# Root finder on POOL ahead of the products of queries and sums, differences of weights at other places, and two more chunks turned on the tensor engine

## The chip, the cores and the metric

The kernel runs on one core of one Trainium2 chip. The metric is the device time of one execution in microseconds (us); the time of a kernel is the median over its runs. The core's engines each work through an instruction queue of their own, in order: TensorE (PE in the profile, with its weight loads as PEld), VectorE (DVE), ScalarE (ACT), GpSimd (POOL), and SyncE (SP), which here only issues DMAs.

## The reference

The input is x of 4 sequences of 2048 positions with 512 features, in float32. Two layers are added to it, each behind a layer norm.

- Attention: `xn = layernorm(layernorm(x)) * ln_g + ln_b`, then queries, keys and values `xn @ W_qkv + b_qkv`, and a gate `sigmoid(layernorm(x) @ W_gate + b_gate)`, divided by its mean over the features. Queries and keys are multiplied by the gate, cut into 16 heads of 32, and turned into `relu(.)**2 + 1e-5`. The attention is linear and causal: at each position the state grows by `k v^T` and the sum of keys by `k`; the output is `q @ state / (q @ sum + 1e-5)`, and then `@ W_proj + b_proj`.
- Feed-forward: `P = layernorm(x) @ U1` (rank 128), `H = gelu(P @ V1 + b1)` (2048 wide), `Q = H @ U2`, and `x + Q @ V2 + b2`.

## The kernel before, in words

The 8192 positions are cut into 64 chunks of 128 (`NC`); chunk c is a tile of 128 positions by 512 features. 16 chunks make a sequence (`SEQ`). The order of the work on every engine is written out by hand: `tc.manual_schedule()` keeps the order in which the program issues it, and waits between engines come from the data and from the tiles' buffers. What is issued earlier on an engine's queue runs earlier on that engine, and a waiting instruction holds all behind it.

After a start in which chunks 0 to 3 are treated by themselves, the main loop takes two chunks in each of 30 steps, c = 4, 6, ..., 62, with e = c - 1 the odd chunk of the pair before. A step issues, in this order:

1. `gates_and_values(c, ...)`: gates and values of chunks c and c + 1. Products of a pair are made with seven half products instead of eight (`half_product`, the matmuls of L426), for which sums and differences of the activations (`combinations`, `combos`, on POOL) and differences of the weights (`difference`, L1014, slots T1 to T4 of the tiles `wgv`, `wqk` and `wp`) are needed.
2. `scores_in_step(e)`: 32 small products (L618) and four masks on VectorE (`a`, L628).
3. `queries_and_keys(c, ...)`: queries and keys of the pair, their squares on ACT, their turning to features first: a transpose in blocks of 32 on VectorE (L286, `blocks_q`, `blocks_k`), a DMA to DRAM (L302) and DMAs back (L307), all through SP. POOL adds to them at L523, L535 and L570.
4. `pump(1)`: the feed-forward of the pair c - 4, c - 3 is a list of 21 pieces, `rest`, of which `pump` issues some: `down` (L844, `ps_P`, from the tile `x2T`; `pT` at L855), 18 pieces `both(f)` (hidden product L859, gelu on ACT L861, and two pieces later its product into `ps_Q`, L865; the last one copies `ps_Q` to `qs` on VectorE, L878), and two pieces `up` (`ps_u`, L883, x + result at L885, and the output DMA L886).
5. The rest of the attention of e, its output combinations (`outs`, POOL, L756 to L759), and `project_two_in_step(e)`, which ends with the moments of the chunks e - 1 and e (`mv`, L226, L227).
6. `sums_and_products(c)`: VectorE's scan `sums` (L594) over the keys of chunk c, and POOL's product `qsum` of queries and sums (L604).
7. `second_norm([e - 1, e], ...)` on POOL: the factors of the second layer norm of chunks e - 1 and e, and, up to c = 58, also those of the first norm of chunks c + 4 and c + 5. L806 to L810 take the variances from `mv`, `inverse_root_by_steps` (L242 to L250) finds the inverse roots in three rounds of four small instructions, and L260, L261, L357 and L358 make the factors (`shift_f`, `shift_o`, `unscale`). It gives back two closures that are kept in `waiting`.
8. `scores_in_step(c)`, then `denominators_in_step(c)`: POOL's x + bp_row (L982), and VectorE's row from `qsum`: transpose `back` (L640), sum (L642), + eps (L643), reciprocals (L649 to L652), transpose `inv` (L655).
9. `pump(4)`, a closure of `waiting`, `pump(2)`, the other closure. Each normalizes one chunk on ACT (x2, L267), adds b2_row to x on POOL (L824), and turns x2: for the chunks below `NC - 2` as in 3 (`turned_in_quarters`: `blocks_x` on VectorE, the write `dr_x`, four reads into `x2T`), for the last two on TensorE (`features_first`, L276, and an ACT copy, L830); of these the turning is handed back as another closure.
10. The combinations of the next pair on POOL, the remaining pieces of `both`, the rest of the attention of c (products with the state, L690, not for the first chunk of a sequence; with the values, L701; the state's growth, L720; `oT` on VectorE, L664), the pieces `up`, the sums of c + 1 and the first norm of the pair c + 4.

The first step, c = 4, differs: x2 of chunks 0 and 1 are normalized inside `queries_and_keys` (`normalized_first`, behind its first VectorE addition, L504), and the sums of chunk 3 are made inside it too. Ahead of the loop the differences of `wgv` are made on POOL between the projection of chunk 0 and the rest of the attention of chunk 1, and those of `wp` behind the projection of chunk 1. Behind the loop chunk 63, the feed-forward of chunks 60 and 61, the projection of chunks 62 and 63, and their feed-forward follow.

Of the kernel before, what the change touches and what calls it, by code (L numbers as in the profile page):

```python
# [60 lines left out]
def tile_linear_attention_block(  # L61
# [19 lines left out]
    nc = tc.nc  # L81
# [213 lines left out]
    def transfers_back():  # L295
        while back:
            back.pop(0)()
# [137 lines left out]
    def gates_and_values(c, s, meanwhile):  # L435

        a, b = xlT_of[c], xlT_of[c + 1]
        lo, hi = slice(0, NH), slice(NH, NK)
        ps1 = bank(f"ps_g_{c}")
        half_product(ps1, a[:, lo], wgv, B11)  # L440
        t1 = temp(f"g1_{c}")
        nc.scalar.copy(t1, ps1)
        ps2 = bank(f"ps_gu_{c}")
        half_product(ps2, s[:, 1], wgv, T2)
        u2 = temp(f"gu2_{c}")
        nc.vector.tensor_add(u2, ps2, t1)
        ps5 = bank(f"ps_g_{c + 1}")
        half_product(ps5, s[:, 2], wgv, T3)
        u3 = temp(f"gu3_{c}")
        nc.vector.tensor_add(u3, ps5, u2)  # L450
        meanwhile()
        half_product(ps1, a[:, hi], wgv, B21, more=True)
        g0 = new_gate(c)
        gate_input(c, g0, ps1)
        done = [sigmoid_of(c, g0)]
        half_product(ps5, b[:, hi], wgv, T4, more=True)
        g1 = new_gate(c + 1)
        nc.vector.tensor_add(g1, ps5, u2)
        gate_input(c + 1, g1, g1)
        done.append(sigmoid_of(c + 1, g1))  # L460


        loaded = work.tile([P, 1], F32, tag="loaded", name=f"loaded_{c}")
        nc.scalar.activation(loaded, eps_col, AF.Gelu_apprx_tanh)
        ps3 = bank(f"ps_gt_{c}")
        half_product(ps3, s[:, 0], wgv, T1)
        t5 = temp(f"g5_{c}")
        nc.vector.tensor_add(t5, ps3, bqkv_row[:, 2 * D : 3 * D])  # L468
        ps4 = bank(f"ps_v_{c}")
        half_product(ps4, s[:, 3], wgv, B22)  # L470
        v0, v1 = new_values(c), new_values(c + 1)
        nc.vector.tensor_add(v0, ps4, t5)
        nc.gpsimd.tensor_add(v1, u3, t5)  # L473
        nc.gpsimd.tensor_add(v0, v0, u2)
        for n, g in enumerate((g0, g1)):
            gate_factor(*done[n])
            gates[c + n] = g, done[n][1]
        values[c], values[c + 1] = v0, v1
# [108 lines left out]
            bias=eps_col,  # L587
        )

    def sums_of(c, kT, qT):  # L590

        sums = work.tile([P, NK, P + 1], F32, tag="sums", name=f"sums_{c}")
        flat = "p g t -> p (g t)"
        nc.vector.tensor_tensor_scan(  # L594
            sums.rearrange(flat),
            keep.rearrange(flat),
            kT.rearrange(flat),
            0.0,
            ALU.mult,
            ALU.add,  # L600
        )
        state["sums"] = sums
        qs = work.tile([P, NK, P], F32, tag="qsum", name=f"qsum_{c}")
        nc.gpsimd.tensor_mul(  # L604
            qs.rearrange("p k (i t) -> p k i t", t=DH),
            qT.rearrange("p i k t -> p k i t"),
            sums[:, :, 1 : P + 1].rearrange("p k (i t) -> p k i t", t=DH),
        )
        return qs
# [190 lines left out]
    def second_norm(chunks, mv, others=(), mv_others=None):  # L800

        at = slice(chunks[0] % NJ, chunks[-1] % NJ + 1)
        name = str(chunks[0])
        n, m = len(chunks), len(others)
        v = variances(n + 2 * m, f"f{name}")
        nc.gpsimd.tensor_scalar_add(v[:, 0:n], mv[:, at, 1], EPS)  # L806
        if others:
            var = mv_others[:, others[0] % NJ : others[-1] % NJ + 1, 1]
            nc.gpsimd.tensor_scalar_add(v[:, n : n + m], var, EPS)
            nc.gpsimd.tensor_scalar(  # L810
                v[:, n + m :], var, 1.0 + EPS, EPS * EPS, ALU.mult, ALU.add
            )
        rs = inverse_root_by_steps(v, "rs_f", name)
        norm = normalizer(mv[:, at, 0], rs[:, 0:n], f"f{name}", nc.gpsimd)
        if others:
            both_factors(others, mv_others, v[:, n:], rs[:, n:], nc.gpsimd)

        def normalize(n, c):
            b, j = divmod(c, NP)
            if b not in x2T_of:  # L820
                x2T_of[b] = work.tile([P, NP, NQ, NK, DH], F32, tag="x2T", name=f"x2T_{b}")
            xt = x_of[c]
            x2 = normalized(xt, norm, n, f"x2_{c}")
            nc.gpsimd.tensor_add(xt, xt, b2_row)  # L824
            to = x2T_of[b][:, j]
            if c < NC - 2:
                turned_in_quarters(x2, to, f"x2_{c}")
                return None

            return lambda: nc.scalar.copy(  # L830
                to.rearrange("p i k t -> p k i t"),
                features_first(x2, f"ps_x2_{c}").rearrange("p k (i t) -> p k i t", t=DH),
            )

        return [lambda n=n, c=c: normalize(n, c) for n, c in enumerate(chunks)]
# [60 lines left out]
    def pump(n):  # L896
        for _ in range(min(n, len(rest))):
            rest.pop(0)()
# [68 lines left out]
    def new_keys_in_step(c):  # L967
        kT = new_keys(c)
        keys_of(kT, pairs[c][2])
        keys[c] = kT, None  # L970

    def sums_and_products(c):
        if c not in keys:
            new_keys_in_step(c)
        kT = keys[c][0]
        keys[c] = kT, sums_of(c, kT, pairs[c][1])

    def scores_in_step(e):
        return scores_of(e, pairs[e][1], keys[e][0])
# [5 lines left out]
    def rest_of_attention(e, scores, inv):  # L985
        results[e] = weighted(e, scores, pairs[e][1], pairs[e][0], values.pop(e), inv)
# [24 lines left out]
    def difference(w, to, engine):  # L1011

        one, other = {T1: (B12, B11), T2: (B22, T1), T3: (B22, B12), T4: (B21, T2)}[to]
        engine.tensor_sub(w[:, to], w[:, one], w[:, other])  # L1014
# [81 lines left out]
    def scores_of_first():  # L1096
        for turn in turn_xl:
            turn()
        held["scores"] = scores_in_step(0)

    second = queries_and_keys(
        2,
        combos.pop(2),
# [11 lines left out]
    new_keys_in_step(2)  # L1115
    inv = denominators_in_step(1)
    project_in_step(0)
    for to in (T1, T2, T4, T3):
        difference(wgv, to, nc.gpsimd)
    rest_of_attention(1, scores, inv)  # L1120
    sums_and_products(2)
    scores = scores_in_step(2)
    second()
    transfers_back()
    project_in_step(1)
    for to in (T1, T2, T4, T3):
        difference(wp, to, nc.gpsimd)
    inv = denominators_in_step(2)
    waiting += second_norm([0, 1], mv_second)
    rest_of_attention(2, scores, inv)  # L1130
# [2 lines left out]
    for c in range(NJ, NC, 2):  # L1133

        e = c - 1
        for n in (c + 4, c + 5):
            if n < NC:
                load_x(n)
        held = {}

        def denominators():
            held["inv"] = denominators_in_step(e)

        later = c == NJ
        if later:
            gates_and_values(c, combos[c], lambda: new_keys_in_step(e))

            def normalized_first():
                while waiting:
                    waiting.pop(0)()  # L1150
                transfers_back()

            scores = scores_in_step(e)
            second = queries_and_keys(
                c,
                combos.pop(c),
                first=normalized_first,
                queries=lambda: sums_and_products(e),
            )
        else:  # L1160
            gates_and_values(c, combos[c], denominators)
            scores = scores_in_step(e)
            second = queries_and_keys(c, combos.pop(c))

        rest += feed_forward((c - 4) // NP)
        pump(1)
        if later:
            denominators()
        rest_of_attention(e, scores, held["inv"])
        combine_results(e)  # L1170
        features_back()
        second()
        if later:
            for turn in normalize_pair(c + 2):
                turn()
            features_back()
        for n in (c + 4, c + 5):
            first_moments(n)
        pump(4)
        project_two_in_step(e)  # L1180
        transfers_back()
        pump(2)
        sums_and_products(c)
        others = [c + 4, c + 5] if c + 4 < NC else []
        waiting += second_norm([e - 1, e], mv_second, others, mv_first)
        pump(2)


        scores = scores_in_step(c)
        inv = denominators_in_step(c)  # L1190
        pump(4)
        waiting.pop(0)()
        pump(2)
        waiting.pop(0)()
        transfers_back()
        if c + 2 < NC:
            combine(c + 2)
        pump(len(rest) - NP)
        rest_of_attention(c, scores, inv)
        if c + 2 < NC:  # L1200
            pump(len(rest))
            sums_and_products(c + 1)
        for turn in normalize_pair(c + 4):
            turn()
# [76 lines left out]
```

## Time and profile before

| | |
|---|---|
| median of 3 runs | 1830.09 us (1827.73 to 1830.84) |
| the profiled execution: its own time | 1826.79 us |
| the profiled execution: span in the profile | 1825.0 us |
| granted clock of TensorE, mean over the span | 0.997 |
| busy: PE, PEld, DVE, ACT, POOL | 97%, 62%, 72%, 36%, 46% |
| chain that ended last | PE 91%, DVE 4%, ACT, DMA, POOL and issue 1% each |
| one step of the loop, `ps_u` (L883) to `ps_u` | 55.7 us |
| one with the first chunk of a sequence | 55.1 us |

A line of a timeline reads: start in us from the span's beginning, duration, engine, line of the kernel, operation, output <- inputs, shape, how many were merged; in brackets the idle time of the engine ahead of it and what the profile names as its end. TensorE's matmuls are pipelined: 0.59 us stands beside a pair of `ps_h` products, and the next pair starts 0.43 us later. So a loss is read from the distance of the starts. A table of groups gives, behind the bar, the busy time, the mean duration in ns, and the idle time ahead of the group with what ended most of it.

### The profile page before, as it was taken

The numbers are of one execution on the slowest core, as the hardware profiler recorded it, in microseconds if no ns is written. First come the engines' busy times: TensorE is split into PE (matmuls) and PEld (weight loads), VectorE is DVE, ScalarE is ACT, GpSimd is POOL, SyncE is SP. The second block draws the span as 40 slices with busy tenths as digits, with TensorE's granted clock in tenths as the row PEclk, the third lists the DMA queues.
The fourth block names the chain that finished last, engine by engine and source line by source line (L and its number), as shares of the span: only waits on it lengthen the run. The fifth ranks groups of instructions, "written<-read, shape, count | busy, mean of one in ns | idle before, by whom it ended". The sixth has DMA issues, their size and how long they took to land.

```text
span 1825.0 us, 35492 instructions
## 1 busy us (share of the span) xinstructions
PE 1776.5 (97%) x13112; PEld 1133.1 (62%) x13112; DVE 1320.5 (72%) x2579; ACT 659.8 (36%) x1203; POOL 834.6 (46%) x1397
## 2 busy tenths in 40 slices
PE   9989999999999999999999999999999999999998
PEld 4545666656666556666566665566655666655667
DVE  7877777777777777677777777776777777777762
ACT  4323433333333334333333333333333333333333
POOL 3574553444553445544545534455435445344441
PEclk9999999999999999999999999999999999999999
DMA  7123322323323333223233233232233332332220
GB/s 229 60 93 99 111 91 82 102 88 103 105 85 90 99 92 110 92 86 100 87 101 116 77 93 99 87 111 96 84 98 88 99 116 76 94 99 75 87 82 24
DMA packets 286129, 173.79 MB, mean 95 GB/s; under 512 B 134654, under 2 KB 235518, under 8 KB 285828
## 3 DMA queue, kind: packets, MB, share of 16 engines
q1 hardware_dynamic: 284894, 171.51, 30.4%
q8 instruction: 104, 1.70, 0.4%
q14 instruction: 69, 0.57, 0.1%
q10 hardware_dynamic: 1062, 0.01, 0.0%
HBM read 89.68 MB, written 81.79 MB: 94 GB/s over the span
## 4 chain that ended last, share of the span: by engine, by line
PE 91%; DVE 4%; ACT 1%; issue 1%; DMA 1%; POOL 1%; SPq 0%; ACTq 0%; DVEq 0%; POOLq 0%
PE ps_Q L865 13%; PE ps_h L859 12%; PE ps_q L426 11%; PE ps_g L426 11%; PE ps_a L618 4%; PE ps_u L883 3%; PE ps_pt L426 3%; PE ps_p L426 3%; PE ps_t L426 3%; PE ps_k L426 3%; PE ps_v L426 3%; PE ps_u L426 3%; PE ps_gt L426 3%; PE ps_pv L426 3%; PE ps_P L844 3%; PE ps_gu L426 3%
## 5 line engine op out<-in xcount | busy, mean ns | idle before, releaser
L861 ACT ACTIVATE h<-ps_h,b_col 128x256 f32<-128x256 f32 x512 | 227.5, 468 | 288.2 <-PE ps_h L859 288.1
L865 PE MATMUL ps_Q<-h,u_sb 128*128 128x256 f32 x1024 | 304.7, 388 | 25.4 <-ACT h L861 25.4
L859 PE MATMUL ps_h<-pT,v_sb 128*128 128x256 f32 x1024 | 300.5, 385 | 1.6 <-DVE pT L855 1.6
L865 PEld LDWEIGHTS ps_Q<-h,u_sb 128*128 128x128 f32 x1024 | 186.2, 189 | 79.8 <-ACT h L861 57.6
L604 POOL TENSOR_TENSOR qsum<-qT,sums 128x512 f32<-128x512 f32 x64 | 75.4, 1178 | 339.5 <-DVE sums L594 333.1
L859 PEld LDWEIGHTS ps_h<-pT,v_sb 128*128 128x128 f32 x1024 | 189.5, 190 | 32.1 <-DVE pT L855 2.9
L426 PE MATMUL ps_q<-wqk,xlT 128*128 128x512 f32 x372 | 177.9, 601 | 0.0
L628 DVE TENSOR_TENSOR a<-ps_a,causal 128x512 f32<-128x512 f32 x256 | 158.3, 680 | 23.8 <-PE ps_a L618 23.8
L426 PE MATMUL ps_g<-wgv,xlT 128*128 128x512 f32 x360 | 166.2, 597 | 3.6 <-DVE gu L450 3.6
L523 POOL TENSOR_TENSOR u<-u,t 128x512 f32<-128x512 f32 x32 | 40.7, 1272 | 214.2 <-DVE t L521 214.2
L570 POOL TENSOR_SCALAR k<-k 128x512 f32<-128x512 f32 x64 | 96.3, 1505 | 82.9 <-DVE blocks_k L286 82.9
L473 POOL TENSOR_TENSOR v<-gu,g 128x512 f32<-128x512 f32 x30 | 38.1, 1271 | 208.1 <-DVE g L468 208.1
L426 PEld LDWEIGHTS ps_g<-wgv,xlT 128*128 128x128 f32 x360 | 68.7, 191 | 90.2 <-issue 85.2
L426 PEld LDWEIGHTS ps_q<-wqk,xlT 128*128 128x128 f32 x372 | 68.1, 189 | 78.3 <-issue 53.1
L405 ACT ACTIVATE gate<-gate 128x512 f32<-128x512 f32 x64 | 40.3, 630 | 192.7 <-DVE gate L401 192.7
L494 ACT ACTIVATE t<-t,rg 128x512 f32<-128x512 f32 x32 | 23.1, 722 | 215.7 <-DVE t L492 215.7
L226 DVE BATCH_NORM_STATS2 st<-x 128x6 f32<-128x512 f32 x128 | 86.5, 676 | 8.4 <-DMA x<-in_L_attn_x_dram 6.2
L498 ACT ACTIVATE k<-u,rg 128x512 f32<-128x512 f32 x64 | 45.7, 714 | 120.8 <-DVE u L492 120.1
L618 PEld LDWEIGHTS ps_a<-qT,kT 32*128 32x128 f32 x2048 | 63.6, 186 | 33.7 <-issue 31.8
L982 POOL TENSOR_TENSOR x<-x,bp_row 128x512 f32<-128x512 f32 x64 | 81.8, 1278 | 0.0
L824 POOL TENSOR_TENSOR x<-x,b_row 128x512 f32<-128x512 f32 x64 | 80.1, 1274 | 0.9 <-ACT x L267 0.9
L594 DVE TENSOR_TENSOR_SCAN sums<-keep,kT 128x516 f32<-128x516 f32 x64 | 78.5, 1227 | 0.3 <-ACT kT L583 0.3
(196 smaller groups left out, 3607.6 us busy)
## 6 DMA issues: line engine op xcount, KB each, us to landing
x<-in_L_attn_x_dram SPq DMA_DIRECT2D x64, 256.0 KB
dr_q<-blocks_q SPq DMA_DIRECT2D x64, 256.0 KB
dr_k<-blocks_k SPq DMA_DIRECT2D x64, 256.0 KB
qT<-dr_q SPq DMA_DIRECT2D x256, 64.0 KB
kq<-dr_k SPq DMA_DIRECT2D x256, 64.0 KB
out_dram<-x SPq DMA_DIRECT2D x64, 256.0 KB
dr_x<-blocks_x SPq DMA_DIRECT2D x62, 256.0 KB
x2T<-dr_x SPq DMA_DIRECT2D x248, 64.0 KB
```

What stands on the lines that cost most here:

```text
L226: nc.vector.bn_stats(st, src)
L426: nc.tensor.matmul(ps, stationary[:, k, :], w[:, slot, k, :], start=(k == 0 and not more), stop=(k == NH - 1), skip_group_check=True,)
L570: nc.gpsimd.tensor_scalar_add(k, k, EPS)
L594: nc.vector.tensor_tensor_scan(sums.rearrange(flat), keep.rearrange(flat), kT.rearrange(flat), 0.0, ALU.mult, ALU.add,)
L604: nc.gpsimd.tensor_mul(qs.rearrange("p k (i t) -> p k i t", t=DH), qT.rearrange("p i k t -> p k i t"), sums[:, :, 1 : P + 1].rearrange("p ...
L618: nc.tensor.matmul(ps[r][:, bass.ts(g, P)], kT[rows, g, 1 : P + 1], qT[rows, :, g, :], start=True, stop=True,)
L628: nc.vector.tensor_tensor(a, ps[r].rearrange("p (g t) -> p g t", t=P), causal.unsqueeze(1).to_broadcast([P, NK, P]), ALU.mult,)
L824: nc.gpsimd.tensor_add(xt, xt, b2_row)
L859: nc.tensor.matmul(ps, v1_sb[:, 0, bass.ts(f, P)], held["p"], start=True, stop=True)
L861: nc.scalar.activation(h, ps, AF.Gelu_apprx_tanh, bias=b1_col[:, f : f + 1])
L865: nc.tensor.matmul(held["q"], u2_sb[:, f, :], held["h"].pop(f), start=(f == 0), stop=(f == NF - 1))
L982: nc.gpsimd.tensor_add(x_of[e], x_of[e], bp_row)
```

## The change

The change moves work, and puts two more chunks on another way.

- `sums_of` and `sums_and_products` take a function `meanwhile`, called between the scan and the product `qsum`. In the main loop `second_norm` is issued there: on POOL the root finder and the norm factors now stand ahead of `qsum` instead of behind it.
- In `normalize` the bound `NC - 2` becomes `NC - 4`: chunks 60 and 61 are turned on TensorE and copied by ACT. In the loop the closures handed back are called behind the last pieces of `both`; for all chunks below 60 there are none.
- T1, T2 and T4 of `wgv` are made on POOL ahead of `queries_and_keys(2, ...)`. T3 stays where all four were, since it takes the place of the weights that the values of chunks 0 to 3 are made with.
- The differences of `wp` are made inside `queries_and_keys(4, ...)`, where x2 of chunks 0 and 1 were normalized; these are now normalized, and their transfers back issued, ahead of `scores_in_step(3)`.

```diff
--- before.py
+++ after.py
@@ -587,7 +587,7 @@
             bias=eps_col,
         )
 
-    def sums_of(c, kT, qT):
+    def sums_of(c, kT, qT, meanwhile=None):
 
         sums = work.tile([P, NK, P + 1], F32, tag="sums", name=f"sums_{c}")
         flat = "p g t -> p (g t)"
@@ -600,6 +600,8 @@
             ALU.add,
         )
         state["sums"] = sums
+        if meanwhile:
+            meanwhile()
         qs = work.tile([P, NK, P], F32, tag="qsum", name=f"qsum_{c}")
         nc.gpsimd.tensor_mul(
             qs.rearrange("p k (i t) -> p k i t", t=DH),
@@ -823,7 +825,7 @@
             x2 = normalized(xt, norm, n, f"x2_{c}")
             nc.gpsimd.tensor_add(xt, xt, b2_row)
             to = x2T_of[b][:, j]
-            if c < NC - 2:
+            if c < NC - 4:
                 turned_in_quarters(x2, to, f"x2_{c}")
                 return None
 
@@ -969,11 +971,11 @@
         keys_of(kT, pairs[c][2])
         keys[c] = kT, None
 
-    def sums_and_products(c):
+    def sums_and_products(c, meanwhile=None):
         if c not in keys:
             new_keys_in_step(c)
         kT = keys[c][0]
-        keys[c] = kT, sums_of(c, kT, pairs[c][1])
+        keys[c] = kT, sums_of(c, kT, pairs[c][1], meanwhile)
 
     def scores_in_step(e):
         return scores_of(e, pairs[e][1], keys[e][0])
@@ -1098,6 +1100,8 @@
             turn()
         held["scores"] = scores_in_step(0)
 
+    for to in (T1, T2, T4):
+        difference(wgv, to, nc.gpsimd)
     second = queries_and_keys(
         2,
         combos.pop(2),
@@ -1115,16 +1119,13 @@
     new_keys_in_step(2)
     inv = denominators_in_step(1)
     project_in_step(0)
-    for to in (T1, T2, T4, T3):
-        difference(wgv, to, nc.gpsimd)
+    difference(wgv, T3, nc.gpsimd)
     rest_of_attention(1, scores, inv)
     sums_and_products(2)
     scores = scores_in_step(2)
     second()
     transfers_back()
     project_in_step(1)
-    for to in (T1, T2, T4, T3):
-        difference(wp, to, nc.gpsimd)
     inv = denominators_in_step(2)
     waiting += second_norm([0, 1], mv_second)
     rest_of_attention(2, scores, inv)
@@ -1144,17 +1145,19 @@
         later = c == NJ
         if later:
             gates_and_values(c, combos[c], lambda: new_keys_in_step(e))
-
-            def normalized_first():
-                while waiting:
-                    waiting.pop(0)()
-                transfers_back()
+            while waiting:
+                waiting.pop(0)()
+            transfers_back()
+
+            def differences():
+                for to in (T1, T2, T4, T3):
+                    difference(wp, to, nc.gpsimd)
 
             scores = scores_in_step(e)
             second = queries_and_keys(
                 c,
                 combos.pop(c),
-                first=normalized_first,
+                first=differences,
                 queries=lambda: sums_and_products(e),
             )
         else:
@@ -1180,22 +1183,28 @@
         project_two_in_step(e)
         transfers_back()
         pump(2)
-        sums_and_products(c)
         others = [c + 4, c + 5] if c + 4 < NC else []
-        waiting += second_norm([e - 1, e], mv_second, others, mv_first)
+
+        def norms():
+            waiting.extend(second_norm([e - 1, e], mv_second, others, mv_first))
+
+        sums_and_products(c, norms)
         pump(2)
 
 
         scores = scores_in_step(c)
         inv = denominators_in_step(c)
         pump(4)
-        waiting.pop(0)()
+        turns = [waiting.pop(0)()]
         pump(2)
-        waiting.pop(0)()
+        turns.append(waiting.pop(0)())
         transfers_back()
         if c + 2 < NC:
             combine(c + 2)
         pump(len(rest) - NP)
+        for turn in turns:
+            if turn:
+                turn()
         rest_of_attention(c, scores, inv)
         if c + 2 < NC:
             pump(len(rest))
```

## The prediction

> **What bounds the kernel now.** I read the page's busy shares first, then its table of groups for TensorE's idle time, then the timelines of all engines through one step, because TensorE is busy 97% and only its gaps can be won or widened. Page, shares and groups (the last columns are idle time ahead of the group and what ended it):
>
> ```profile
> PE 1776.5 (97%) x13112; PEld 1133.1 (62%) x13112; DVE 1320.5 (72%) x2579; ACT 659.8 (36%) x1203; POOL 834.6 (46%) x1397
> ...
> L865 PE MATMUL ps_Q<-h,u_sb 128*128 128x256 f32 x1024 | 304.7, 388 | 25.4 <-ACT h L861 25.4
> ```
>
> The largest idle time is 25.4 us: products `ps_Q` that wait for a gelu, once in each of the 30 steps (0.86 to 0.89 us in nearly all of the first 28, 0.36 and 0.35 in the last two). One step in the timelines, TensorE, then POOL, ACT, VectorE:
>
> ```profile
> 706.90 0.59 PE L859 MATMUL ps_h<-pT,v_sb 128*128 128x256 f32 x2
> 708.37 0.70 PE L865 MATMUL ps_Q<-h,u_sb 128*128 128x256 f32 x2 [0.87 <-ACT h L861]
> ...
> 712.77 1.98 PE L883 MATMUL ps_u<-v_sb,qs 128*128 128x512 f32 x4
> ```
>
> ```profile
> 701.03 1.18 POOL L604 TENSOR_TENSOR qsum<-qT,sums 128x512 f32<-128x512 f32 x1 [8.59 <-DVE sums L594]
> 702.17 0.23 POOL L806 TENSOR_SCALAR v_f<-mv 128x2 f32<-128x2 f32 x1
> ...
> 706.88 0.23 POOL L261 TENSOR_SCALAR shift_f<-shift_f 128x2 f32<-128x2 f32 x1
> ...
> 707.96 1.28 POOL L982 TENSOR_TENSOR x<-x,bp_row 128x512 f32<-128x512 f32 x1
> ```
>
> ```profile
> 707.14 0.81 ACT L267 ACTIVATE x<-x,shift_f,rs_f 128x512 f32<-128x512 f32 x1 [1.66 <-DVE inv L655]
> ```
>
> ```profile
> 699.55 0.18 DVE L227 BATCH_NORM_AGGREGATE mv<-st 128x2 f32<-128x6 f32 x1
> 699.71 1.23 DVE L594 TENSOR_TENSOR_SCAN sums<-keep,kT 128x516 f32<-128x516 f32 x1
> ...
> 704.11 0.70 DVE L640 STREAM_TRANSPOSE back<-qsum 128x512 f32<-128x512 f32 x1
> ```
>
> The moments are there at 699.73, but POOL waits for the scan, multiplies (`qsum`), and only then finds roots. ACT starts x2 at 707.14, 0.03 us behind the end of `shift_f` (the releaser printed, `inv`, was not it), and two gelus stand behind it. Matmul pairs go every 0.433 us: 706.90 to 708.37 loses 1.04, the restart 0.10, the last gather 0.12. Without the wait, `ps_u` could start at 712.77 - 1.27 = 711.50.
>
> **Root finder ahead of qsum (28 steps, c = 4 to 58).** The root and its factors take 707.96 - 702.17 = 5.79 us. VectorE's scan is already running when the root may start, and POOL has been held by such an instruction:
>
> ```profile
> 107.34 0.54 POOL L249 TENSOR_SCALAR newton_t<-newton_t 128x2 f32<-128x2 f32 x1
> ...
> 107.07 0.75 DVE L401 SCALAR_TENSOR_TENSOR gate<-gate,unscale,bg_row 128x512 f32<-128x512 f32 x1
> ...
> 97.60 2.62 POOL L1014 TENSOR_TENSOR wp<-wp 128x512 f32<-128x512 f32 x2
> ...
> 97.69 1.22 DVE L643 TENSOR_SCALAR den<-den 128x16 f32<-128x16 f32 x1
> ```
>
> A root instruction of 0.20 took 0.54 and ended 0.06 behind a VectorE operation with two SBUF inputs. At 28.62 a POOL difference of 2.36 took 3.40, one at 86.96 behind a scan 3.32. So the first instruction (L806) ends 0.06 behind the scan's 700.94, at 701.00 instead of 702.40: the root gains 1.40, not the 2.35 that mv alone would allow. The other end: no hold, 2.35. I take the hold.
>
> `shift_f` then ends at 705.71, x2 runs 705.74 to 706.55, the second 707.23 to 708.04, each gelu is ready before its product: the 1.27 go. What is late next is **qsum**, with two POOL additions behind it and VectorE's whole row behind it: start 707.96 - 1.40 = 706.56, end E = 707.74 (1.18).
> Then, with pitches of the rows at 95 to 100 us: L640 at E + 0.04, L642 + 0.75, L643 + 0.72, which is E + 1.51. POOL is then in L824 (start E - 0.04 + 1.23 = E + 1.19, two SBUF inputs, 1.27). The fence shows what L643 does then: 1.22 instead of 0.17, to 0.03 behind the end of POOL's first `wp` operation (1.27); at 82.78 it took 0.45, again to 0.03 behind a POOL operation's end. So L643 ends at E + 2.49 (free: E + 1.68). L655 follows at E + 3.17, the two block transposes at + 0.63 each (E + 3.80, E + 4.43), the copy `qs` E + 5.05 to E + 5.48, `ps_u` 0.04 later: E + 5.52 = **713.26, against 712.77 before**. The old wait of 1.27 turns into a new one of 1.76 ahead of `ps_u`, +0.49 a step. In c = 16, 32, 48 no state products stand ahead of `ps_u` (period 55.13 for 55.70), so it had been 0.57 earlier: +1.06. Sum 25 x 0.49 + 3 x 1.06 = **+15.4**. c = 60 has a shorter root (4.39): qsum 1707.51, `ps_u` 1714.21 for 1714.61, **-0.4**.
> Bounds from those rows: root held, L643 free: 712.47, -0.30 a step; root free, L643 held: 712.31, -0.46; both free: 711.50, -1.27.
>
> The rule that speaks here is the Trainium skill's, "SBUF — State Buffer", section "Who interferes with whom": a VectorE instruction with two SBUF inputs contends with a GpSimd one that reads SBUF, and the second to issue blocks fully. By it both holds stand. By it the sum is the forecast's; by the odd row alone it would be the first rival's. That row: at 686.30 such a VectorE operation ran at its usual 0.69 while POOL's L570 was under way (685.77 to 687.28).
>
> Hidden: x2's writes and reads through SP go some 3 us later; SP is free from 724.1 to 737.0, and `ps_P` reads x2T only at 739.9. Cover gone, each would add its lateness to `ps_P`.
>
> **Features of chunks 60, 61 on TensorE (c = 62).** Gone: two block transposes, two writes, eight reads, and the wait they end with:
>
> ```profile
> 1777.00 1.96 PE L844 MATMUL ps_P<-x2T,u_sb 128*128 128x256 f32 x8 [2.41 <-DMA out_dram<-x]
> ```
>
> Added: eight transposes, 0.87 at the pitch of those at 1799.31, about 0.95 with the switch, and two ACT copies (0.59) ahead of kT, which then ends at 1769.5, before the scores need it (1770.0). The step's own wait (0.35, 0.75 with its edges) goes too. Of the 2.41 some 0.1 stays as the switch: -0.75 + 0.95 - 2.3 = **-2.1**; bounds -3.1 (transposes hidden) and 0.
>
> **Differences of wgv (T1, T2, T4) ahead of the second pair's queries.** Three of 2.36 us on POOL from 50.47, free there until 56.34. The copy is cheap, the cover is not: VectorE runs its norm factors there (L260, L357, L358: two SBUF inputs; L347, L261: one small input) and POOL's operations take turns with such ones (at 17.59 to 20.98 L919 took 1.1 each instead of 0.75, POOL's 1.17 instead of 0.73). Each turn can cost up to 2.2 us. L401 moves from 52.02 to between 55.5 and 58, so L504 and the products at 55.94 wait 2 to 4.4, and ACT's chain to `ps_t` (61.31) up to 5. Bounds 0 (no turn lost) and +7 (5.2 and a half-clock window); I take **+4.5**.
>
> **Taken out behind it.** POOL's four differences (84.54 to 95.00) held qsum, so VectorE waited 2.98 at 96.22, and TensorE:
>
> ```profile
> 102.81 3.50 PE L426 MATMUL ps_g<-wgv,xlT 128*128 128x512 f32 x4 [3.59 <-DVE gu L450]
> ...
> 125.60 3.00 PE L844 MATMUL ps_P<-x2T,u_sb 128*128 128x256 f32 x8 [2.54 <-DMA dr_q<-blocks_q]
> ```
>
> With T3 alone left, `gu` is ready at 98.5, before TensorE wants it at 99.06: 3.75 and 1.6 of half clock go. But kT(3) still lands at 102.7, so ACT's sigmoids end near 104.9, x2 of chunks 0, 1 at 107.8, and VectorE now has their block transposes ahead of the four masks: masks 108.4 to 110.8, L504 to 111.5, the products behind it at 111.5 instead of 114.31: only 2.8 are kept. `ps_P` would come at 120.1, x2T by about 119.6, so its 2.54 and its half-clock window (1.7) go: 125.6 - 120.1 = 5.5, and 1.7 more, less about 1 for `wp`'s four differences (5.06), which now run at 109.6 to 114.7 against L492 and the scan: **-6**; bounds -8 and -3.
>
> **Sum**: 15.4 - 0.4 - 2.1 + 4.5 - 6.0 = +11.4 on the profiled execution's 1826.79 (span 1825.0 and 1.79 around it), 1838.2. The median of the runs shown, 1830.09, lies 3.30 above that execution; carried to it, 1841.5.
>
> **Rivals.**
> - Root not held by the scan (for: one odd row at 686.30, and only one small root operation ever seen held; against: the rows above): 25 x -0.46 + 3 x 0.11 = -11.2, c = 60 -0.7, the rest -3.6: **1814.6**, faster. It decides from E below 707.25. With L643 free instead: -6.7 - 0.7 - 3.6, **1819**.
> - Neither held: 28 x -1.27 = -35.6, **1790**. Against: four held rows.
> - Half clock at the new gap of 1.76. In the trace's record of the granted clock (0.57 on the mean of 102 to 106 and of 126 to 130), windows of 3.41 us went to half speed behind ones with 1.09, 0.14 and 0.87 us of products; the one from 1775.03, with 1.44, did not. The new gap leaves 1.65, but partly of small tiles. If it triggered whenever a window holds the gap whole (1.65 of 3.41 phases): 28 x 0.48 x 1.7 = +23, **1864**.
>
> The Trainium skill ("TensorE: Matmul & The Clock Gate", section "HAM oscillation — how this bites in real kernels") sets the limit at idle gaps above about 3.4 us, by which this rival costs nothing; the gap of 2.3 us behind 75.2 did slow the clock.
>
> **Chances.** Both holds, as forecast: 0.64 (1831 to 1851 by the front's bounds and 0.15 a step). Root free 0.14, L643 free 0.07, both free 0.07, half clock 0.08. The range 1812 to 1852 takes in the first three. Faster by over 0.2% (3.7 us, about what a measurement can tell here) 0.28, within it 0.05, slower 0.67.
>
> **What would show it.** `ps_Q` without waits; a wait of TensorE ahead of `ps_u` L883 for `qs`, near 1.8 us; L806 stretched to about 1.2 behind the scan; L643 near 1.0 in every even step; no wait of `ps_P` near 1775; VectorE's L260 or L261 stretched near 52 us. Wrong if L806 shows 0.23 beside a running scan, if L643 stays at 0.17, or if `qs` is there before TensorE wants it.

## The result, and the profile after

The changed kernel takes **1844.53 us** (median of 4 runs, 1841.43 to 1846.93) against 1828.91 of the kernel before in the same comparison: ratio **1.0084**, 95% interval 1.0063 to 1.0105: slower by 0.84%. The forecast was 1841.5, slower, in a range of 1812 to 1852. The profiled execution took 1846.02 (span 1844.2, mean granted clock 0.994), 19.2 more than that of before.

In the changed kernel most lines have moved by two: the root starts at L808 (was L806), x + b2_row is L826, qsum L606, the row's sum, eps and turn are L644, L645 and L657, x + bp_row is L984, the differences are L1016, `ps_u` is L885 and `ps_Q` L867.

The page of the changed kernel, busy shares, chain, and groups:

```profile
PE 1773.4 (96%) x13120; PEld 1138.4 (62%) x13120; DVE 1338.4 (73%) x2577; ACT 665.6 (36%) x1205; POOL 859.7 (47%) x1397
...
PE 70%; DVE 12%; POOL 6%; DMA 5%; issue 4%; SPq 2%; ACT 2%; DVEq 0%; POOLq 0%; ACTq 0%
...
L867 PE MATMUL ps_Q<-h,u_sb 128*128 128x256 f32 x1024 | 298.5, 383 | 1.4 <-ACT h L863 1.4
...
L808 POOL TENSOR_SCALAR v_f<-mv 128x2 f32<-128x2 f32 x32 | 34.7, 1084 | 228.1 <-DVE mv L227 228.1
...
L885 PE MATMUL ps_u<-v_sb,qs 128*128 128x512 f32 x128 | 65.7, 637 | 45.8 <-DVE qs L880 45.7
```

The 25.4 us of idle time ahead of `ps_Q` are 1.4 now, so the part that was meant to go has gone. In its place 45.7 us stand ahead of `ps_u`, which had no wait in these steps. The root's first small operation takes 1084 ns on the mean where it took 0.23 us. The chain that ended last was PE for 91%, and is PE for 70%, the rest being VectorE, POOL and what they wait for: the loop now runs through the row of denominators.

The step that stood at 699.55 in the prediction, in the changed kernel, POOL, then VectorE, then PE:

```profile
710.37 1.14 POOL L808 TENSOR_SCALAR v_f<-mv 128x2 f32<-128x2 f32 x1 [7.38 <-DVE mv L227]
...
715.98 0.22 POOL L261 TENSOR_SCALAR shift_f<-shift_f 128x2 f32<-128x2 f32 x1
...
717.09 1.17 POOL L606 TENSOR_TENSOR qsum<-qT,sums 128x512 f32<-128x512 f32 x1
718.22 1.27 POOL L984 TENSOR_TENSOR x<-x,bp_row 128x512 f32<-128x512 f32 x1
719.45 1.26 POOL L826 TENSOR_TENSOR x<-x,b_row 128x512 f32<-128x512 f32 x1
```

```profile
710.10 0.18 DVE L227 BATCH_NORM_AGGREGATE mv<-st 128x2 f32<-128x6 f32 x1
710.26 1.23 DVE L594 TENSOR_TENSOR_SCAN sums<-keep,kT 128x516 f32<-128x516 f32 x1
...
718.29 0.71 DVE L642 STREAM_TRANSPOSE back<-qsum 128x512 f32<-128x512 f32 x1 [3.55 <-POOL qsum L606]
719.04 0.69 DVE L644 TENSOR_REDUCE den<-back 128x16 f32<-128x512 f32 x1
719.76 0.98 DVE L645 TENSOR_SCALAR den<-den 128x16 f32<-128x16 f32 x1
720.78 0.20 DVE L651 RECIPROCAL inverse<-den 128x8 f32<-128x8 f32 x1
...
723.26 0.39 DVE L880 COPY qs<-ps_Q 128x256 f32<-128x256 f32 x1
...
732.94 0.17 DVE L645 TENSOR_SCALAR den<-den 128x16 f32<-128x16 f32 x1
```

```profile
723.70 1.98 PE L885 MATMUL ps_u<-v_sb,qs 128*128 128x512 f32 x4 [1.55 <-DVE qs L880]
```

Read it from the top. The scan runs from 710.26 to 711.49, and L808, which starts beside it, ends at 711.51. The root then goes its usual way, and qsum, which used to stand ahead of it, ends at 718.26. VectorE has waited 3.55 us for it. Its sum (L644) runs at its usual time beside POOL's additions, but the eps (L645, 16 elements in each lane) takes 0.98 beside L826 and ends 0.03 behind the first addition of L826 (719.45 + 1.26 = 720.71); the reciprocals behind it take 0.20 again. The line at 732.94 is the same eps for the odd chunk of the step, with nothing running on POOL: 0.17. Over the whole trace L645 took 0.17 to 0.18 in the 30 cases with POOL at rest; in 32 others a POOL TENSOR_TENSOR was under way, and each of them ended 0.03 to 0.04 behind that operation. `qs` comes behind all that, and `ps_u` 1.55 us too late.

### The profile page after: what moved, and what is told of

Its sections match the earlier page's. It is cut to its first block, busy times and chain, and to the rows that moved or that the text cites. A ratio compares the mean times of both kernels' runs of the same rounds, so it can differ in the third digit from the quotient of the medians.

```text
span 1844.2 us, 35489 instructions
## 1 busy us (share of the span) xinstructions
PE 1773.4 (96%) x13120; PEld 1138.4 (62%) x13120; DVE 1338.4 (73%) x2577; ACT 665.6 (36%) x1205; POOL 859.7 (47%) x1397
## 4 chain that ended last, share of the span: by engine, by line
PE 70%; DVE 12%; POOL 6%; DMA 5%; issue 4%; SPq 2%; ACT 2%; DVEq 0%; POOLq 0%; ACTq 0%
PE ps_q L426 11%; PE ps_g L426 11%; PE ps_h L861 6%; PE ps_Q L867 4%; PE ps_u L885 4%; PE ps_t L426 3%; PE ps_k L426 3%; PE ps_u L426 3%; PE ps_gt L426 3%; PE ps_gu L426 3%; PE ps_v L426 3%; PE ps_pt L426 3%; DMA kq<-dr_k 2%; PE ps_p L426 2%; PE ps_a L620 2%
## 5 line engine op out<-in xcount | busy, mean ns | idle before, releaser
L867 PE MATMUL ps_Q<-h,u_sb 128*128 128x256 f32 x1024 | 298.5, 383 | 1.4 <-ACT h L863 1.4
L867 PEld LDWEIGHTS ps_Q<-h,u_sb 128*128 128x128 f32 x1024 | 189.1, 190 | 41.9 <-ACT h L863 18.7
L808 POOL TENSOR_SCALAR v_f<-mv 128x2 f32<-128x2 f32 x32 | 34.7, 1084 | 228.1 <-DVE mv L227 228.1
L570 POOL TENSOR_SCALAR k<-k 128x512 f32<-128x512 f32 x64 | 96.2, 1503 | 85.8 <-DVE blocks_k L286 85.8
L606 POOL TENSOR_TENSOR qsum<-qT,sums 128x512 f32<-128x512 f32 x64 | 75.3, 1176 | 103.1 <-DVE sums L594 96.6
L642 DVE STREAM_TRANSPOSE back<-qsum 128x512 f32<-128x512 f32 x64 | 45.2, 706 | 103.8 <-POOL qsum L606 103.7
L885 PE MATMUL ps_u<-v_sb,qs 128*128 128x512 f32 x128 | 65.7, 637 | 45.8 <-DVE qs L880 45.7
L498 ACT ACTIVATE k<-u,rg 128x512 f32<-128x512 f32 x64 | 45.7, 714 | 122.8 <-DVE u L492 122.0
```

The costliest lines, as they stand in the source:

```text
L498: nc.scalar.activation(sq, t, AF.Square, scale=rg)
L570: nc.gpsimd.tensor_scalar_add(k, k, EPS)
L606: nc.gpsimd.tensor_mul(qs.rearrange("p k (i t) -> p k i t", t=DH), qT.rearrange("p i k t -> p k i t"), sums[:, :, 1 : P + 1].rearrange("p ...
L642: nc.vector.transpose(back.rearrange("p g t -> p (g t)"), qs.rearrange("p g t -> p (g t)"))
L867: nc.tensor.matmul(held["q"], u2_sb[:, f, :], held["h"].pop(f), start=(f == 0), stop=(f == NF - 1))
L885: nc.tensor.matmul(ps, held["qs"][:, bass.ts(j, P)], v2_sb[:, 0, :], start=True, stop=True)
```

## The experiments

Each comparison has its own runs of the kernel before (medians 1827.7 to 1828.4). A difference in us that stands with a ratio is the ratio's excess times 1828.

**1. The root ahead, and nothing else.**

```diff
-        sums_and_products(c)
-        waiting += second_norm([e - 1, e], mv_second, others, mv_first)
+        def norms():
+            waiting.extend(second_norm(...))
+        sums_and_products(c, norms)
```

> The kernel before with one part of the change: in the loop the root finder stands ahead of qsum, all else as before. Theory (the root is held by the scan, and qsum, the + eps row held by a POOL addition and the copy qs then come late for ps_u): ps_u waits about 1.5 us in each of 28 steps, the period goes from 55.70 to 56.08, by 0.95 where a sequence begins, and the three steps there fall to half clock once each (1.7): 25 x 0.38 + 3 x 0.95 + 3 x 1.7 - 1 for the last two steps, +16, about 1845. Rival (the loss lies in the moved differences at the start, and the root itself is neutral or a gain because the gelu's wait goes): 1800 to 1830.

Measured: 1847.47 us (1846.87 to 1847.82), ratio 1.0108 [1.0091, 1.0125]: the root's new place alone costs 19.7 us, a little more than the whole change. Its profile has the new wait (45.6 us ahead of `ps_u`), two half-clock windows inside the loop, and at the tail one wait of 6.7 us of `ps_P` for x2T of chunks 60 and 61, with 6.8 us at half clock, of which 3.2 lie in the wait itself. That one is the loss of cover that the prediction named for the later x2; it is only met at the tail, and the part that turns these chunks on TensorE takes it away.

**2. Everything but the root.** The changed kernel with `second_norm` behind qsum again.

> The changed kernel with the root finder put back behind qsum: the differences at their new places and chunks 60 and 61 on TensorE stay. Theory: the gelu waits of 0.87 are back in all steps, no wait ahead of ps_u; start +4, tail -2: 1831, within 3 us of the kernel before. Rival (the start makes the loss): 1840 or more.

Measured: 1828.81 us (1827.04 to 1831.28), ratio 1.0004 [0.9994, 1.0013]: no difference. The waits of `ps_Q` are back (25.8 us). So the whole loss is the root's place, and the other parts come out at nothing together.

**3. The same wait taken away from the other side: x2 later.** The gelu was late because x2 stood ahead of it on ACT, waiting for the factors. Here the root stays behind qsum, and the first x2 is issued two pieces of the feed-forward later.

```diff
-        pump(4)
+        pump(6)
         waiting.pop(0)()
         pump(2)
```

> The kernel before, with only the order on ACT changed: six pieces of the feed-forward instead of four are issued ahead of the first normalization x2, so that the gelus of hidden products 12 and 13 stand ahead of it. Root and qsum stay in the old order. Theory (the old 0.87 us wait is two gelus behind an x2 that waits for the root, and nothing else): the wait goes without qsum being late, 1.2 us a step, 30 steps: 1795 (1790 to 1800). Rival (another wait takes its place: x2's block transposes now reach VectorE later and hold qs, or the late b2 additions hold the combinations of the next pair): 1815 to 1830, with the wait of ps_u or ps_gu to show it.

Measured: 1795.79 us (1793.5 to 1796.83), ratio 0.9823 [0.9809, 0.9838]. The loop has no wait of `ps_Q` and none of `ps_u`: in the traces the steps c = 6 to 58 take 1.25 us less each than before. So the wait that the change takes away is worth in the loop what the prediction put on it (1.27 a step), and there it can be had without another wait in its place. The price comes at the tail:

```profile
1742.66 3.75 PE L844 MATMUL ps_P<-x2T,u_sb 128*128 128x256 f32 x8 [3.73 <-DMA out_dram<-x]
```

`ps_P` of chunks 60 and 61 waits 3.73 us for 2.41 before, and 10.24 us from 1740.91 on are at half clock. In this profiled execution that gives back 5.1 of the 35.7 us that had been gained up to `ps_u` of c = 62.

**4. Scan and qsum early.** They are issued between the two halves of the projection, where the keys of chunk c are already there, so that qsum is done before the last moments arrive, and the root meets no scan.

```diff
-        project_two_in_step(e)
+        project_two_in_step(e, lambda: sums_and_products(c))
         transfers_back()
         pump(2)
-        sums_and_products(c)
```

> The kernel before, with the scan and qsum of chunk c issued between the last two moments of the projection, so that VectorE's scan is over before the root finder starts and qsum is done ahead of it. Theory (a running scan holds the root's first POOL instruction; qsum must not stand behind the root): L806's counterpart takes 0.23 us instead of 1.1, shift_f is ready about 1.2 us earlier against the gelus than before, no wait ahead of ps_Q nor of ps_u: 1795 to 1805. Rival (the first instruction is long for another reason, say its wait for the moments): it still shows about 1.1 us. Risk that is neither: the keys have not landed when ACT comes to them, and ACT's copy for the projection or the gelus wait, 1820 to 1850.

Measured: 1793.7 us (1792.67 to 1796.34), ratio 0.9816 [0.9801, 0.983]. POOL in one step of this kernel:

```profile
686.97 1.53 POOL L604 TENSOR_TENSOR qsum<-qT,sums 128x512 f32<-128x512 f32 x1 [6.45 <-DVE sums L594]
689.03 0.22 POOL L808 TENSOR_SCALAR v_f<-mv 128x2 f32<-128x2 f32 x1 [0.53 <-DVE mv L227]
```

The same L808 takes 0.22 where no scan runs beside it. This shows the first hold: it is the scan, not the operation or the wait for `mv`. One step of experiment 1 says the same with the root in its new place: there the scan began late, at 1154.71; L808, just ahead of it, took 0.22, and the next small operation, L811, took 1.23. (qsum itself is stretched, 1.53 for 1.17, beside VectorE's L795 with two SBUF inputs; it has time.) At the tail this kernel pays as experiment 3 does: `ps_P` waits 3.78 there, with 10.24 us at half clock.

**5. The second hold, taken out.** The changed kernel without its line of + eps.

```diff
-        nc.vector.tensor_scalar_add(den, den, EPS)
```

> The changed kernel without the addition of 1e-5 to the denominators (VectorE's TENSOR_SCALAR of 128x16, L645), so the output lacks that term. Theory: in the changed kernel this small one-input operation takes 0.98 us in every even step because POOL's addition L826 is under way; the reciprocals behind it run at 0.20 beside the same kind of addition, so without it they start about 1.02 us earlier, qs and ps_u too: 28 x -1.02 = -28.6, and the wait ahead of ps_u shrinks from 1.55 to about 0.5, so the three half-clock windows of the steps c = 16, 32, 48 (1.70 each) go as well: about 1811 us against 1844.5 of the changed kernel. Rival: POOL then holds the next small VectorE operation (a reciprocal) in its place: no change, 1842 to 1847, reciprocals of about 1 us.

Measured: 1812.12 us (1807.88 to 1814.15), ratio to before 0.9905 [0.9891, 0.9919]. VectorE in this kernel (its lines behind the removed one stand one lower):

```profile
709.42 0.69 DVE L644 TENSOR_REDUCE den<-back 128x16 f32<-128x512 f32 x1
710.14 0.20 DVE L650 RECIPROCAL inverse<-den 128x8 f32<-128x8 f32 x1
```

The reciprocal starts where L645 stood, at 0.20, and POOL's addition runs from 709.82 beside it. No half-clock window is left inside the loop. `ps_u` still waits, 16.9 us in all and about 0.5 in most steps, since qsum still stands behind the root. So this one operation of 16 elements in each lane, 0.17 us when free, is worth 32 us of the changed kernel's time: without it the changed kernel is 0.95% faster than the kernel before, which has the addition, and not 0.84% slower. The run leaves the eps out altogether, so 0.17 and the pitch of a step are in that figure as well as the hold's 0.8.

**6 to 8. The other parts, one at a time.** Turning chunks 60 and 61 on TensorE (the edit of `NC - 2` and of the closures):

> The kernel before with only chunks 60 and 61 turned on TensorE. Theory (the changed kernel's trace, where the tail became 2.3 us shorter): TensorE's wait of 2.41 us ahead of ps_P near 1775 goes, eight transposes come in: -2.3 us, 1826 against 1828.4 of before. Rival: the transposes and copies cost what the wait was worth: within 1 us of before.

Measured: 1825.63 us (1825.26 to 1826.7), ratio 0.9987 [0.9978, 0.9995]: -2.4 us (-4.0 to -0.9), as the theory had it.

The three differences of `wgv` at their earlier place:

> The kernel before with only T1, T2 and T4 of wgv made ahead of the queries of the second pair. Theory: +4.1 us near 52 us (VectorE's norm factors stretched to about 2 us each), and the wait of 3.59 us ahead of ps_g near 102.8 goes with its half-clock window (3.75 + 1.6): about -1.2, 1827. Rival: what goes at 102.8 comes back at the wait of ps_P near 125, because kT of chunk 3 lands later by what was lost at 52 us: +3 to +5, 1831 to 1833.

Measured: 1828.91 us (1824.87 to 1834.11), ratio 1.0007 [0.9999, 1.0016]: +1.3 us (-0.2 to +2.9), which doesn't reach the theory's -1.2 and isn't told from nothing. Nor is the rival's +3 reached. The waits of TensorE in the start, in this kernel's trace, speak for the rival's mechanism:

```profile
60.18 3.78 PE L426 MATMUL ps_q<-wqk,xlT_early 128*128 128x512 f32 x4 [3.64 <-DVE t L504]
...
129.18 1.97 PE L844 MATMUL ps_P<-x2T,u_sb 128*128 128x256 f32 x8 [3.17 <-DMA dr_q<-blocks_q]
```

The wait of 3.59 at 102.8 has gone and a new one of 3.64 stands at 60.2; and `ps_P`, which waited 2.54, waits 3.17 at 129.2.

The differences of `wp` at their later place:

> The kernel before with only the differences of wp moved into the queries of the first step, where the second norm of chunks 0 and 1 was applied, and that norm ahead of the scores of chunk 3. Theory: the block transposes of x2 now stand ahead of the four masks on VectorE and x2 itself is not earlier (ACT reaches it at 110.0 as before), so masks, L504 and the third product of the queries come 1.2 us later; x2T is there some 2 us earlier, so the wait of 2.54 ahead of ps_P near 125.6 shrinks to about 0 with its half-clock window: together -2, 1826. Rival: the later masks cost as much as ps_P gains, or open a half-clock window of their own: 0 to +3, 1828 to 1831.

Measured: 1829.04 us (1827.71 to 1832.38), ratio 1.0008 [0.9999, 1.0016]: +1.5 us (-0.2 to +2.9), on the rival's side, but not told from nothing either. The wait of `ps_P` near 125 is gone from this trace too, and waits of 0.75 (`ps_q`, 116.42), 1.39 (`ps_Q`, 133.15) and 1.81 (`ps_pt`, 140.84) have come in its place.

**9 and 10. What the experiments point to.** Experiment 4 with chunks 60 and 61 turned on TensorE:

> Two parts together on the kernel before: scan and product qsum issued as soon as the keys of chunk c are there, inside the projection of chunks e - 1 and e (1793.7 by itself), and chunks 60 and 61 turned on TensorE. Theory: in the first part alone TensorE waits 3.8 us for x2T of chunks 60 and 61 and then runs 10.2 us at half clock; both go, the eight transposes add 0.95: 3.8 + 5.1 - 0.95 = 7.9, so 1786. Rival: the half clock of that profile is not in most executions, as with the 2.4 us wait of before, so that only the wait goes: 1790 to 1792.

Measured: 1790.30 us (1790.02 to 1790.44), ratio 0.9793 [0.978, 0.9807]; the rival's number. The half clock at the tail was in the profile of experiment 4, and that was its slowest execution; 3.4 us come from the median.

The same with the x2 of experiment 3:

> As the other kernel of this pair, and x2 of chunk e - 1 normalized two feed-forward pieces later on ACT. Theory: no ps_Q product waits for a gelu any more once the scan is early, so two pieces later change nothing in the steps: within 1 us of the other kernel. Rival: the later x2 makes x2T late for ps_P, some tenths of a us in each step: 10 us or more slower.

Measured: 1789.81 us (1789.38 to 1790.05), ratio 0.9791 [0.9777, 0.9804], as the theory had it: once the scan is early, moving x2 changes the time by 0.5 us. Both are **2.1% faster than the kernel before** (1.9 to 2.2), and use one part of the change.

## Why the prediction was right, and where it was not

**The main step held, both holds with it.** L808 stretches to 1.14 behind the scan (predicted about 1.2). L645 takes 0.98 (predicted 0.98 from E + 1.51 to E + 2.49). `ps_Q`'s waits go, `ps_u` waits 1.55 (predicted 1.76). From `mv` to `ps_u` it is 13.42 us after and 13.04 before: **+0.38 a step, predicted +0.49**, and in c = 16, 32 and 48 +0.95, predicted 1.06. Of the 0.11, 0.08 lie in VectorE's row behind qsum (5.44 from its end to `ps_u`, predicted 5.52) and 0.03 ahead of it. The first hold is shown by an experiment that takes the holder away: the root at 0.22 beside no scan (experiment 4). For the second, experiment 5 takes the held instruction away and shows what the hold costs; that POOL's addition is the holder is read from the rows, 0.17 with POOL at rest and 32 ends just behind the end of a POOL operation.

The prediction named a rule for both holds, from the Trainium skill's "SBUF — State Buffer", section "Who interferes with whom". In the form in which it is quoted, with two SBUF inputs on VectorE, the rule covers the scan, but not L643, which has one. The same section names `tensor_scalar` between SBUF tensors among the VectorE operations that can take the port pair shared with GpSimd though they have one input, and says that `tensor_reduce` on trn2 never does. The rows agree: beside POOL's additions L645, a TENSOR_SCALAR, took 0.98, the TENSOR_REDUCE ahead of it 0.69. Against the rule stands what the prediction called one odd row. It is no single row: in each of the twelve traces (before, changed, ten experiments) VectorE's L492, with two SBUF inputs, began 64 times while POOL's L570 was under way, and took its usual 0.69 every time, as here in the changed kernel's trace (POOL, then VectorE, two operations in one line):

```profile
696.33 1.51 POOL L570 TENSOR_SCALAR k<-k 128x512 f32<-128x512 f32 x1 [2.57 <-DVE blocks_k L286]
...
696.86 1.29 DVE L492 SCALAR_TENSOR_TENSOR u<-u,gate 128x512 f32<-128x512 f32 x2
```

L570 is a TENSOR_SCALAR with one input in SBUF; every POOL operation that held VectorE's eps row was a TENSOR_TENSOR with two. Here the measurement decides: not every POOL operation that reads SBUF holds a VectorE operation with two inputs there. On the root's hold the row says nothing, since there VectorE's scan is the first of the two.

**The half-clock rival did happen, in three steps.** PE of the changed kernel in the first chunk of a sequence, c = 16:

```profile
497.66 2.63 PE L885 MATMUL ps_u<-v_sb,qs 128*128 128x512 f32 x4 [2.13 <-DVE qs L880]
500.08 2.98 PE L426 MATMUL ps_g<-wgv,xlT 128*128 128x512 f32 x4
```

No state products stand ahead of `ps_u` there, so the wait is 2.13, and the record of the granted clock has 0.5 from 498.86 to 502.28; c = 32 and 48 have such a window too. `ps_g` takes 2.98 for 1.88. Each costs 1.70: **+5.1** that the forecast had put at nothing and left to the rival as a whole (+23, at 0.48 of the 28 steps). In the 25 steps with waits of 1.53 to 1.75 it never came.

**The step that failed is "taken out behind it", -6.** It gained 0.15. From the first products of the second pair on, the changed kernel is 4.08 behind (predicted +4.5, the term of `wgv`; the 0.57 by which its first transposes start later in the trace is left out here and below): VectorE's norm factors, 0.15 to 0.17 each before, in the trace of the changed kernel:

```profile
51.30 2.06 DVE L347 TENSOR_SCALAR v<-mv 128x4 f32<-128x4 f32 x1
...
53.94 1.83 DVE L260 TENSOR_TENSOR shift_o<-mv,rs_o 128x4 f32<-128x4 f32 x1
55.80 0.17 DVE L261 TENSOR_SCALAR shift_o<-shift_o 128x4 f32<-128x4 f32 x1
55.88 2.32 DVE L357 TENSOR_TENSOR unscale<-rs_o 128x4 f32<-128x4 f32 x1
```

At `ps_u` of c = 4 it is still 3.9 behind, without the 0.4 of that step's own new wait. The waits at 102.81 and 125.60 went, as forecast, and their half-clock windows with them. What the forecast missed: it let kT of chunk 3 land at 102.7 as before, although its own term of `wgv` made everything ahead of it later. ACT, VectorE and PE of the changed kernel:

```profile
108.62 0.72 ACT L583 ACTIVATE kT<-kq,eps_col 128x512 f32<-128x512 f32 x1 [9.27 <-DMA kq<-dr_k]
...
111.99 1.51 ACT L267 ACTIVATE x<-x,shift_f,rs_f 128x512 f32<-128x512 f32 x2
```

```profile
112.83 1.42 DVE L286 STREAM_TRANSPOSE blocks_x<-x 128x512 f32<-128x512 f32 x2 [1.87 <-ACT x L267]
114.17 2.45 DVE L630 TENSOR_TENSOR a<-ps_a,causal 128x512 f32<-128x512 f32 x4
116.53 0.67 DVE L504 TENSOR_TENSOR t<-ps_q,bqkv_row 128x512 f32<-128x512 f32 x1
```

```profile
117.26 3.78 PE L426 MATMUL ps_q<-wqk,xlT 128*128 128x512 f32 x4 [3.06 <-DVE t L504]
```

kT lands 5.9 later (TensorE's work on the second pair stood 4.7 later in the trace; where the rest comes from was not followed), x2, the masks and L504 follow one behind the other, and the products that were forecast at 111.5 start at 117.26, behind a new wait of 3.06 and with two windows of half clock. What was gained ahead is lost here. Experiments 2, 6, 7 and 8 say the same in time: the two moves of differences cost 1.3 and 1.5 by themselves, the tail gives 2.4, which makes +0.4, and the three together measured +0.7. The start as a whole lost, where a gain of 1.5 was forecast.

**The tail was right**: -2.3 in the traces and -2.4 as an experiment, predicted -2.1; c = 60 gained 0.56, predicted 0.4.

**So the total came out near by luck, by errors that cancel.** In the profiled executions: steps c = 6 to 58 +16.9 (11.8 of gaps and 5.1 of half clock; predicted 15.4 for one step more, c = 4), c = 60 and tail -2.9 (predicted -2.5), start +3.9 (predicted -1.5), c = 4's own +0.4, and 0.9 of other differences at the two ends, together 19.2; predicted 11.4. The medians lie 15.6 apart, 3.6 less than the profiled executions. The direction doesn't rest on that: experiments 1 and 2 put the loss in the root's place alone. Their sum, 19.7 + 0.7, is 5 us above the 15.4 of the whole, within their intervals together. The traces have a reason for it: from `ps_u` of c = 62 to the next `ps_u` it is 37.97 us in experiment 1, 31.96 before and 29.49 in the changed kernel, so experiment 1 loses 6.0 at the tail to the late x2T, and the turning on TensorE takes that away.

**What stays open**: the size of the start's loss, 3.9 in the profiled execution and 2.8 as the sum of experiments 7 and 8, whose times move by some us between executions (1824.87 to 1834.11 in experiment 7); and why VectorE's L492 is not held beside POOL's L570. That L570 has one input is what sets it apart in these rows, but no run gave it a second one.

## What to carry to other kernels

When a late instruction is moved ahead of another on an in-order queue, the one it overtakes is the next candidate: follow that one's whole chain to the engine that sets the time, before counting the gain. Where two engines hold one another, an operation's price depends on what runs beside it: 0.17 us can be 0.98, and a row that is hidden can become the bound through its smallest member. Better than to exchange two pieces of work is to find the time in which one of them could already run: the scan had its keys some microseconds earlier, and issued there it cost nothing in the loop and gave 1.8%. The faster loop then met a late transfer at the tail; with that put right too it was 2.1%.

## What the runs showed of the hardware

- **Half clock depends on where a gap falls.** The slow spells last 3.41 us or a multiple, and in each trace they lie on one grid of 3.41 us. TensorE's busy time, as the profile gives it, in every window of that grid, over all twelve traces, tells most of what follows. At full clock, each of the 43 windows with at most 1.42 us of work was followed by one at half clock, and none of the 6207 with 1.76 or more; of the 15 between, 5 were. At half clock, the 14 windows with at most 2.90 us of work were followed by another, the 42 with 2.98 or more by full clock.
- **So the same gap can cost something or nothing.** Waits of 2.13 to 2.16 ahead of `ps_u` in c = 16, 32 and 48 were followed by half clock in 5 of 6 cases (three in the changed kernel, two of three in experiment 1): those five left 1.25 to 1.28 us of work in a window, while the sixth fell across two windows with 1.91 and 2.77. The waits of about 1.55 left 1.85 or more. In the start that many of these kernels share, the wait of 2.35 ahead of `ps_p` near 78 us was followed by half clock in the traces of before and of experiments 1, 3, 4 and 8, and not in those of 6, 9 and 10, so a profile of one execution doesn't tell it for another. At the tail, ahead of `ps_P`, 2.41 (before) and 2.77 (experiment 8) were followed by none, 3.04 (experiment 7), 3.73 (experiment 3) and 3.78 (experiment 4) by three windows, 10.24 us. PE of experiment 4 there, where eight products take 3.75 for 1.96:

```profile
1742.28 3.75 PE L846 MATMUL ps_P<-x2T,u_sb 128*128 128x256 f32 x8 [3.78 <-DMA out_dram<-x]
```

- **A small operation on VectorE can wait for a whole one on POOL, and the other way round**: L645 0.17 free and up to 0.996 held; L808 0.22 free, 1.146 the median; while TENSOR_REDUCE (0.69), RECIPROCAL (0.20) and STREAM_TRANSPOSE (0.71) kept their times beside POOL's additions. So did a still smaller TENSOR_SCALAR of VectorE, L410 with 128x1: in the changed kernel it took 0.13 to 0.15 in all 35 cases in which a POOL TENSOR_TENSOR ran over its whole length.
